# Three expert levels of a perceiver on one code: tokens gathered by expert, four pairs per level, TensorE branching by counts

## The chip, the cores and the metric

The kernel runs on one core of one Trainium2 chip. The metric is the device time of one execution in microseconds. Shown are three runs of the kernel before (672.74, 673.07 and 673.65, median 673.07) and one execution taken by the profiler.

Engines are named by their work: TensorE (PE: matmuls; PEld is its weight loading), VectorE (DVE), ScalarE (ACT), GpSimd (POOL), and SyncE (SP), which issues the transfers.

## The reference, cut to what matters

128 tokens (two batches of 64) of 256 values pass four levels. Each level is cross-attention to a context, then a mixer, then a feed-forward layer of eight experts of which every token uses two, and every part adds its output to x:

```python
x = x + _L1_ffn_ref(_layernorm(x), ...)
x = x + _L2_ffn_ref(_layernorm(x), ...)
x = x + _L3_ffn_ref(_layernorm(x), ...)
```

The feed-forward layer of level 2, for example:

```python
logits = xf @ router_w.T
top_w, top_i = lax.top_k(softmax(logits), 2)
top_w = top_w / sum(top_w)                 # combine[token, expert]
g = einsum('nd,ehd->neh', xf, w_gate)
u = einsum('nd,ehd->neh', xf, w_up)
y = einsum('neh,edh->ned', silu(g) * u, w_down)
out = einsum('ned,ne->nd', y, combine)
```

Level 1 has hidden width 1024, one product with a bias and Gelu (no gate), and an output bias. Level 2 has width 512, gate and up, Silu, no biases. Level 3 has width 1024, gate and up with biases, Silu, an output bias, and a router bias. All is float32. Level 0 (Gelu, dense in both kernels) is not touched.

## The kernel before, in words

All of x lies on 128 partitions, one token each. The stages follow one another: l0x, l0a, l0f, l1x, l1a, l1f, l2x, l2t, l2f, l3x, l3a, l3f (x: cross-attention, a or t: mixer, f: experts). A stage starts with the row normalisation of x and its transposition by TensorE, since TensorE contracts over partitions. `in_written_order` (L283) keeps each engine's instructions in the order of the text; elsewhere a scheduler orders them. Every engine works its own queue in order; SyncE does too, so a transfer whose buffer is not free holds all transfers behind it.

Weights come through a pool of buffers by size (L123): six of 1 MB ("w8"), four of 0.5 MB ("w4"), six small. `weight` (L125) takes the next free buffer and issues the load. `bank` (L88) gives one PSUM bank (512 float32 columns), `two_banks` (L91) a tile of two.

**Dense levels.** l1f (from L1773) and l2f (from L2366) compute all eight experts for all 128 tokens. `gate` (L331) makes the router's logits, the best two and their weights `comb`. For each expert `features` (L383) computes the hidden values turned (features on partitions), weights as the stationary operand; in l1f ScalarE applies Gelu with a bias column (L1784), in l2f ScalarE applies Silu to the gate and VectorE multiplies. `Mix.add` (L374) computes the output product and VectorE adds it, scaled by the token's weight (L378). `later` lets the output product of one expert stand behind the hidden product of the next.

**Gathered level.** l3f uses `experts` (L620). Tokens are sorted by expert into 128 slots per pair (r, r+4): a one-hot matrix `pick` made from the tokens' positions gathers x by a matmul (`gather`, L672), weights are now the moving operand and the gathered tokens the stationary one, so that the hidden values stand with slots on partitions, and `from_slot` (the transposed picks with the tokens' weights) scatters the outputs into one sum `acc` (L712). A pair has 64 slots for each of its experts, as two column tiles of TensorE; if the first expert of the pair has no token, all 128 slots go to the second. TensorE loads that decision from memory (`read_split`, L720) and branches (`by_tiles`, L725) for every hidden product (L643) and output product (L702). The hidden product is done in two halves of 512 columns, each with a gate and a product bank. Both halves lie in the same two tiles of two banks (`room_for_sums`, L631): the low banks of the two tiles are one half, the high banks the other. ScalarE applies Silu (L664), VectorE multiplies, TensorE turns the result (L688). `add_biases` (L653) opens the sums of the next pair with the biases by a small matmul.

Tokens beyond an expert's room go to four overflow blocks of 32 slots. `plan_blocks` (L836) is computed always, and 14 indirect loads on GpSimd always fetch those blocks' weights. Whether they are used is a branch at the end (L955) of TensorE, ScalarE and VectorE on `any_over`, read at L946.

**Constants and fillers.** `Counting` (L525) makes counting matrices with GpSimd and VectorE; it is set up before l3a, as is the negated sum of the router's columns (`less_sums`, TensorE and VectorE), with which the logits can be computed from x before it is normalised. `keep_busy` (L314) issues matmuls without use. Work for later stages is used as a filler too: in l1a and l1f TensorE computes values of level 3's cross-attention from `l3x_wv` (`context_values`, L403/L405), in l2t and l2f keys from `l3x_wk` (L429/L434). l3x_wk holds a "w4" buffer until level 3.

**l1a.** Its chain from the router-like logits to the new x is VectorE's: an addition (L1732), a maximum, ScalarE's exponential (L1735), six products and sums (L1745, L1749), then TensorE's turning of rows (L1756) and the product with x (L1764). TensorE runs fillers beside it.

Of the kernel before, what the change touches and what calls it, by code (L numbers as in the profile page):

```python
# [18 lines left out]
P = 128  # L19
# [18 lines left out]
    ("l1x_bq", 4), ("l1x_bk", 4), ("l1x_bv", 2), ("l1f_b1", 64),  # L38
# [20 lines left out]
def tile_perceiver(ctx: ExitStack, tc: tile.TileContext, i: dict, out: bass.AP):  # L59
# [465 lines left out]
    class Counting:  # L525
# [3 lines left out]
        def __init__(self, pool, biases):  # L529
# [30 lines left out]
            )  # L560

            self.p, self.p32 = p, p32
            self.biases = made(512, "bs")
            nc.sync.dma_start(self.biases, i[biases])

    class Shelf:
# [13 lines left out]
        def whole(self, t, wide):  # L580
            return lambda c, f: t[:, c * wide + f.start : c * wide + f.stop]

        def load(self, r):
            for n in self.order:
                src = i[f"{self.name}_w{n}"]
                _, _, chunks, wide = src.shape
                for j in range(2):
                    t = self.room(self.place(r, j, n), chunks * wide)
                    nc.sync.dma_start(t, src[r + PAIRS * j].rearrange("p c f -> p (c f)"))
                    self.at[r, j, n] = self.whole(t, wide)  # L590

        def fetch(self, blocks, index, index2):

            for j, n in blocks:
                src = i[f"{self.name}_w{n}"]
                _, _, chunks, wide = src.shape
                tag = self.place(OVER, j, n)
                parts = 2 if tag == "halves" else 1
                ts = []
                for k in range(parts):  # L600
                    t = self.room("w4" if parts == 2 else tag, chunks * wide // parts)
                    at = index[:, j : j + 1] if parts == 1 else index2[:, j, k : k + 1]
                    nc.gpsimd.indirect_dma_start(
                        t, None, src.rearrange("e p (k c) f -> (e p k) (c f)", k=parts),
                        bass.IndirectOffsetOnAxis(ap=at, axis=0),
                        bounds_check=8 * P * parts - 1, oob_is_err=False,
                    )
                    ts.append(self.whole(t, wide))
                each = chunks // parts
                self.at[OVER, j, n] = lambda c, f, ts=ts, each=each: ts[c // each](c % each, f)  # L610

    def tiles_of(k):

        if k == OVER:
            return [(slice(j * 32, j * 32 + 32), j) for j in range(4)]
        if k == 0:
            return [(slice(0, P), 1)]
        return [(slice(j * 64, j * 64 + 64), j) for j in range(2)]

    def experts(name, x, consts, shelf, blocks, pool, acc, less_sums, bias, b2):  # L620
        count, width = consts.count, 1024
        from_slot = pool.tile([P, OVER + 1, P], F32, name="from_slot")
        over, over_w = (pool.tile([P, P], F32, name=n) for n in ("over", "over_w"))
        own_over = pool.tile([P, P], F32, name="own_over")
# [3 lines left out]
        xg, hT, y, own, prods = {}, {}, {}, {}, {}  # L628
        low, high = slice(0, 512), slice(512, 1024)

        def room_for_sums():  # L631
            ps, other = two_banks(), two_banks()
            return [
                (ps[:, low], 1, low, 0), (other[:, low], 0, low, 2),
                (ps[:, high], 1, high, 1), (other[:, high], 0, high, 3),
            ]

        def hidden(r, parts, tiles):

            for part, n, f, k in parts:  # L640
                for c in range(2):
                    for s, j in tiles:
                        nc.tensor.matmul(  # L643
                            part[s], xg[r][:, c, s], shelf.at[r, j, n](c, f),
                            start=(r == 0 and c == 0), stop=False,
                            skip_group_check=True,
                        )

        def add_biases(r, parts):
            mine = own_over if r == OVER else own[r]  # L650
            for part, _, _, k in parts:
                e = slice(32 * k, 32 * k + 8)
                nc.tensor.matmul(  # L653
                    part, mine[e], consts.biases[e], start=(r > 0), stop=(r == 0),
                    skip_group_check=True,
                )

        def gates(r, parts):
            if r not in prods:
                prods[r] = pool.tile([P, width], F32, name="m_prod", bufs=2)  # L660
            g = pool.tile([P, width], F32, name="m_g")
            for k, (part, n, f, _) in enumerate(parts):
                if k % 2 == 0:
                    nc.scalar.activation(g[:, f], part, AF.Silu)  # L664
                else:
                    nc.vector.tensor_tensor(prods[r][:, f], part, g[:, f], ALU.mult)

        def gather(r):
            ps = bank()
            mine = over if r == OVER else pick[:, r]  # L670
            for c in range(2):
                nc.tensor.matmul(  # L672
                    ps[:, c * P : (c + 1) * P], xl[:, c * P : (c + 1) * P], mine,
                    start=True, stop=True,
                )
            if r == OVER:
                nc.tensor.transpose(ps[:, 2 * P : 3 * P], over_w, ident)
            xg[r] = pool.tile([P, 2, P], F32, name="m_xg", bufs=2)
            nc.scalar.copy(xg[r].rearrange("p c s -> p (c s)"), ps[:, : 2 * P])
            if r == OVER:  # L680
                nc.scalar.copy(from_slot[:, OVER], ps[:, 2 * P : 3 * P])

        def turn(r, k):
# [9 lines left out]
            if k:  # L693
# [16 lines left out]

        def scatter(r):
            nc.tensor.matmul(  # L712
                acc, from_slot[:, r], y[r], start=False, stop=(r >= PAIRS - 1),
                skip_group_check=True,
            )

        split = {}
# [7 lines left out]
        def by_tiles(r, behind, work):  # L725

            with tc.If(split[r] == 1) as shared:
                with in_written_order(behind):
                    work(tiles_of(1))
            with shared.Else():  # L730
                with in_written_order(behind):
                    work(tiles_of(0))

        with in_written_order() as done:
            ps = bank()
            for c in range(2):
                nc.tensor.transpose(ps[:, c * P : (c + 1) * P], x[:, c * P : (c + 1) * P], ident)
            keep_busy(1)
# [5 lines left out]
            r_ = rstd_of(mv[:, 1:2], 1, AF.Silu)  # L744
# [6 lines left out]
                lg, less_sums, mv[:, 0:1], ps[:, :8], ALU.mult, ALU.add  # L751
            )
            nc.vector.scalar_tensor_tensor(lg, lg, r_, bias, ALU.mult, ALU.add)
# [9 lines left out]
            )  # L763
            diff, th, w = stat(name="g_d"), stat(name="g_t"), stat(2, "top_w")
            nc.vector.tensor_tensor(diff, best[:, 0:1], best[:, 1:2], ALU.subtract)
            nc.scalar.activation(th, diff, AF.Tanh, scale=0.5)
            keep_busy(4)
# [3 lines left out]
            nc.tensor.matmul(ps[:, :8], consts.upto, mask, start=True, stop=True)  # L771
            keep_busy(2)
            one, two = slice(0, PAIRS), slice(PAIRS, 8)
            at_slot = pool.tile([P, 8], F32, name="m_at_slot")
            any_first = pool.tile([P, PAIRS], F32, name="m_any")
            split_at = small.tile([P, PAIRS], U32, tag="split", bufs=1, name="split")
            limit = pool.tile([P, 8], F32, name="m_limit")
            pos, number = (pool.tile([P, 8], F32, name=n) for n in ("m_pos", "m_number"))
            nc.vector.tensor_scalar(split_at, ps[:, 8 : 8 + PAIRS], 0.0, None, ALU.is_gt)
            nc.vector.tensor_scalar(any_first, ps[:, 8 : 8 + PAIRS], 0.0, None, ALU.is_gt)  # L780
            nc.vector.tensor_tensor(pos, ps[:, :8], mask, ALU.mult)
            nc.vector.scalar_tensor_tensor(
                at_slot[:, two], any_first, 64.0, pos[:, two], ALU.mult, ALU.add
            )
            nc.vector.tensor_tensor(at_slot[:, two], at_slot[:, two], mask[:, two], ALU.mult)
            nc.vector.scalar_tensor_tensor(
                at_slot[:, one], pos[:, one], 64.0, pos[:, one], ALU.is_le, ALU.mult
            )

            def picked(r):  # L790
                nc.vector.tensor_scalar(
                    pick[:, r], count, at_slot[:, r : r + 1], None, ALU.is_equal
                )
                nc.vector.scalar_tensor_tensor(
                    pick[:, r], count, at_slot[:, PAIRS + r : PAIRS + r + 1], pick[:, r],
# [3 lines left out]
            picked(0)  # L799
            read_split(0)  # L800
            nc.scalar.copy(number, ps[:, 8:16])
            gather(0)
            nc.vector.tensor_scalar(limit[:, one], any_first, 64.0, None, ALU.mult)
            nc.vector.tensor_scalar(limit[:, two], any_first, -64.0, float(P), ALU.mult, ALU.add)

            def owned(r):
                own[r] = pool.tile([P, P], F32, name=f"own{r}")
# [9 lines left out]
            for r in range(1, PAIRS):  # L817
                picked(r)
                owned(r)
# [6 lines left out]
            wide = pool.tile([P, PAIRS, P], F32, name="m_wide")  # L826
            for t, k in ((slot_w, 0), (wide, PAIRS)):
                for r in range(PAIRS):
                    e = slice(k + r, k + r + 1)
                    nc.vector.tensor_scalar(  # L830
                        t[:, r], count, at_slot[:, e], comb[:, e], ALU.is_equal, ALU.mult
                    )
            nc.gpsimd.tensor_tensor(slot_w, slot_w, wide, ALU.add)
# [1830 lines left out]
```

## Time and profile before

| | us |
|---|---|
| median of three runs | 673.07 |
| profiled execution | 673.79 |
| its span (first to last instruction) | 671.9 |
| l1f: x's transposes to those of l2x | 187.16 to 249.53 |
| l2f: first expert's product to l3x's transposes | 499.14 to 544.50 |
| l3f: first hidden product to the last scatter | 605.98 to 667.16 |

The mean granted clock of TensorE is 0.998. In the profile's lines an operation is told by its line in the kernel, its engine, its tiles (output <- input) and shape, and, in brackets, the idle time of its engine before it and what ended that. TensorE's records overlap each other by their pipelining, so distances are taken between starts. A float32 matmul leaves two matmul records and two weight-load records; TensorE has 4812 of each.

### The profile page before, as it was taken

How to read it: one execution, taken by the hardware profiler on the slowest of the kernel's cores; microseconds unless marked ns; L12 is line 12 of the kernel's file. 1: busy time of each engine (PE TensorE's matmuls, PEld its weight loads, DVE VectorE, ACT ScalarE, POOL GpSimd, SP SyncE). 2: the span in 40 equal slices, each digit the busy share in tenths (PEclk: the TensorE clock that was granted, in tenths of full speed). 3: DMA queues.
4: the chain of work that ended last, by engine and by line, in shares of the span. 5: the costliest groups of instructions: out<-in, count | busy, mean ns of one | idle time of the engine just before them, and what ended most of it. 6: DMA issues, size and time to landing. Idle time of an engine off the chain costs nothing. (4 is left out here: it accounts for less than half of the span.)

```text
span 671.9 us, 11767 instructions
## 1 busy us (share of the span) xinstructions
PE 638.5 (95%) x4812; PEld 506.3 (75%) x4812; DVE 297.8 (44%) x814; ACT 261.1 (39%) x531; POOL 62.6 (9%) x88
## 2 busy tenths in 40 slices
PE   7989999999899999999999989999999999989996
PEld 3547659766589988999997778999979966774443
DVE  5875451278420014554554435634422257755211
ACT  1464461488543332332323515305331159641111
POOL 3450000000000000000000040030000000100043
PEclk9999999999999999999999999999999999999999
DMA  8960025810038885000001300011118840274760
GB/s 285 401 270 1 17 72 199 322 44 1 3 125 299 289 267 210 2 1 1 1 1 58 131 1 1 2 63 63 63 63 301 299 151 2 90 303 186 318 250 10
DMA packets 21367, 86.81 MB, mean 129 GB/s; under 512 B 4080, under 2 KB 8704, under 8 KB 13024
## 3 DMA queue, kind: packets, MB, share of 16 engines
q1 hardware_dynamic: 19040, 85.96, 35.2%
q8 instruction: 41, 0.67, 0.4%
q0 software_dynamic: 2016, 0.01, 0.1%
q14 instruction: 14, 0.11, 0.0%
q10 hardware_dynamic: 256, 0.06, 0.0%
HBM read 98.46 MB, written 0.13 MB: 147 GB/s over the span
## 5 line engine op out<-in xcount | busy, mean ns | idle before, releaser
L1894 PE MATMUL bank<-l2x_ctx,p 128*128 128x193 f32 x256 | 48.1, 327 | 0.0
L378 DVE SCALAR_TENSOR_TENSOR x_new<-bank,comb,x_new 128x256 f32<-128x256 f32 x24 | 11.6, 484 | 80.0 <-PE bank L270 80.0
L1894 PEld LDWEIGHTS bank<-l2x_ctx,p 128*128 128x128 f32 x256 | 40.8, 190 | 0.4
L1547 DVE CUSTOM_DVE_ANT_0 p<-two_banks,zero 128x1024 f32<-128x1024 f32 x32 | 38.6, 1217 | 5.2 <-PE two_banks L1537 5.0
L1555 ACT ACTIVATE p<-p,negmax 128x1024 f32<-128x1024 f32 x32 | 36.9, 1153 | 4.7 <-DVE negmax L1547 4.7
L1843 PE MATMUL two_banks<-l2x_qA,ctxA 128*128 128x128 f32 x256 | 31.9, 278 | 0.0
L1858 DVE TENSOR_REDUCE l2x_mx<-two_banks 128x128 f32<-128x1024 f32 x16 | 19.6, 1224 | 26.6 <-PE two_banks L1850 26.6
L1843 PEld LDWEIGHTS two_banks<-l2x_qA,ctxA 128*128 128x128 f32 x256 | 30.3, 192 | 1.2 <-issue 1.0
L1784 ACT ACTIVATE l1f_hT<-bank,cols 128x128 f32<-128x128 f32 x64 | 18.2, 367 | 32.9 <-PE bank L270 32.9
L270 PEld LDWEIGHTS bank<-xT,l1f_w_sb 128*128 128x128 f32 x256 | 29.7, 192 | 0.6 <-issue 0.3
L270 PE MATMUL bank<-xT,l1f_w_sb 128*128 128x128 f32 x256 | 30.1, 276 | 0.0
L270 PEld LDWEIGHTS bank<-xT,l2f_w_sb 128*128 128x128 f32 x256 | 29.6, 192 | 0.3
L270 PE MATMUL bank<-xT,l2f_w_sb 128*128 128x128 f32 x256 | 29.8, 275 | 0.0
L270 PE MATMUL bank<-l1f_w_sb,l1f_hT 128*128 128x256 f32 x128 | 28.8, 379 | 0.0
L1880 DVE TENSOR_TENSOR p<-two_banks,l2x_shift 128x512 f32<-128x512 f32 x32 | 20.6, 686 | 13.1 <-ACT l2x_shift L1875 13.1
L270 PEld LDWEIGHTS bank<-l1f_w_sb,l1f_hT 128*128 128x128 f32 x128 | 23.8, 190 | 2.9
L1887 ACT ACTIVATE p<-p 128x512 f32<-128x512 f32 x32 | 19.6, 630 | 12.1 <-DVE p L1880 12.1
L1562 PEld LDWEIGHTS two_banks<-ident,p 128*128 128x128 f32 x128 | 13.7, 140 | 11.0 <-ACT pT L1591 9.1
L223 ACT ACT_TABLE_LOAD x16 | 20.5, 1283 | 0.3
L1537 PE MATMUL two_banks<-n_kT,n_qx 32*128 32x512 f32 x128 | 19.2, 640 | 0.0
L1562 PE MATMUL bank<-ident,p 128*128 128x128 f32 x128 | 18.6, 280 | 0.5
L1850 PE MATMUL two_banks<-l2x_qB,ctxB 64*128 64x128 f32 x256 | 18.6, 285 | 0.0
(598 smaller groups left out, 1313.0 us busy)
## 6 DMA issues: line engine op xcount, KB each, us to landing
l1f_w_sb<-in_l1f_w_dram SPq DMA_DIRECT2D x16, 1024.0 KB, 4.8
l3f_w_sb<-in_l3f_w_dram SPq DMA_DIRECT2D x12, 1024.0 KB, 5.3
more_w<-in_l3f_w_dram SPq DMA_DIRECT2D x12, 1024.0 KB, 8.2
l0f_w_sb<-in_l0f_w_dram SPq DMA_DIRECT2D x8, 1024.0 KB, 8.9
l2f_w_sb<-in_l2f_w_dram SPq DMA_DIRECT2D x8, 1024.0 KB, 4.8
l2f_w_sb<-in_l2f_w_dram SPq DMA_DIRECT2D x8, 512.0 KB, 4.5
xh<-in_ctx_dram SPq DMA_DIRECT2D x8, 192.0 KB, 6.0
l2x_ctx<-in_ctx_dram SPq DMA_DIRECT2D x1, 1536.0 KB, 8.0
```

The lines of the kernel that those rows point to most:

```text
L223: nc.scalar.activation(junk, behind, func, scale=0.0)
L270: nc.tensor.matmul(dst, lhsT, rhs, start=(k == 0), stop=(k == len(pairs) - 1))
L1537: nc.tensor.matmul(sc[u][:, n * 512 : (n + 1) * 512], qx[c, n][rows_, b].rearrange("p h q -> p (h q)"), kT[c, b][rows_, n, :], start=True, ...
L1547: nc.vector.tensor_tensor_reduce(p[u], sc[u], zero.to_broadcast([P, NK]), -1.0, 3.0e38, ALU.add, ALU.min, least)
L1555: nc.scalar.activation(p[u], p[u], AF.Exp, bias=sc[u], scale=-1.0, accum_out=total[u // 4][:, u % 4 : u % 4 + 1],)
L1562: nc.tensor.transpose(ps[:, kc * P : (kc + 1) * P], p[u][:, (4 * k + kc) * P : (4 * k + kc + 1) * P], ident,)
L1843: nc.tensor.matmul(sc[k][:, n, t, :], ctxA[:, b, n, t * P : (t + 1) * P], qA[:, j, b].rearrange("p h q -> p (h q)"), start=(t == 0), stop= ...
L1850: nc.tensor.matmul(sc[k][:, n, t, :], ctxB[half[n], b, t * P : (t + 1) * P], qB[half[n], j, b].rearrange("p h q -> p (h q)"), start=False, ...
L1858: nc.vector.tensor_reduce(mx[k], sc[k].rearrange("p n t q -> p q (n t)"), AX.X, ALU.max)
L1880: nc.vector.tensor_tensor(p[k][:, n], sc[k][:, n], shifts[k].unsqueeze(1).to_broadcast([P, 4, P]), ALU.add,)
L1887: nc.scalar.activation(p[k][:, n], p[k][:, n], AF.Exp)
L1894: nc.tensor.matmul(po[k][:, : CD + 1], p[k][:, kc // 4, kc % 4, :], crows[:, b * 8 + kc, :], start=(kc == 0), stop=(kc == 7),)
```

## The change

- l1f and l2f use `experts` as l3f does. A `Level` tells the activation, the width, whether there is a gate, and the biases. In l1f and l2f a pair is shared 64/64 when its first expert has more than 32 tokens, else 32/96, the latter in four 32-column tiles (three of them for the second expert). l3f keeps 64/64 or whole.
- The sums of a half lie in the two banks of one tile, the second half's in another tile. `acc` is an ordinary bank.
- `Counting` and the router sums of levels 1 to 3 are made before and in l1a instead of l3a; the sums' matmul and negation are written behind two fillers and ahead of the addition that starts l1a's chain.
- The overflow plan, its loads and its products are all inside two branches at the end of each level.
- Weights of l2x, l3x and l3f's first pair are asked for earlier in the text, behind the shelf of l1f or l2f. l1f has four 1 MB buffers more ("more").

```diff
-    def tiles_of(k):
-        if k == OVER:
-            return [(slice(j * 32, j * 32 + 32), j) for j in range(4)]
-        if k == 0:
-            return [(slice(0, P), 1)]
-        return [(slice(j * 64, j * 64 + 64), j) for j in range(2)]
+    class Level:
+        def room_for_sums(self):
+            low, high = slice(0, 512), slice(512, 1024)
+            ps = two_banks()
+            if self.width == 512:
+                return [[(ps[:, low], 1, low, 0), (ps[:, high], 1, high, 1)]]
+            if not self.gated:
+                return [[(ps[:, low], 1, low, 0), (ps[:, high], 1, high, 1)]]
+            other = two_banks()
+            return [
+                [(ps[:, low], 1, low, 0), (ps[:, high], 0, low, 2)],
+                [(other[:, low], 1, high, 1), (other[:, high], 0, high, 3)],
+            ]
+        def tiles_of(self, equal):
+            if equal:
+                return [(slice(j * 64, j * 64 + 64), j) for j in range(2)]
+            if self.least == 0:
+                return [(slice(0, P), 1)]
+            return [(quarter_tile(j)[0], min(j, 1)) for j in range(4)]
...
-            ps, other = two_banks(), two_banks()
-            return [
-                (ps[:, low], 1, low, 0), (other[:, low], 0, low, 2),
-                (ps[:, high], 1, high, 1), (other[:, high], 0, high, 3),
-            ]
...
-        with tc.If(more == 0) as none:
-            pass
-        with none.Else():
-            with in_written_order():
-                gather(OVER)
...
+        given = None
+        for part in (lambda _: over_features(), over_outputs):
+            with tc.If(some == 0) as none:
+                pass
+            with none.Else():
+                with in_written_order():
+                    given = part(given)
...
+        def router_sums(self):
+            ps = bank()
+            at = SMALL["l1f"][0]
+            accumulate(ps[:, :24], [(ones, routers[:, c, at : at + 24]) for c in range(2)])
+            nc.vector.tensor_scalar(self.less_sums, ps[:, :24], -1.0, None, ALU.mult)
...
         steps(fill[1])
         steps(fill[2], 2)
+        consts.router_sums()
...
-        mix = Mix(x, gate(xlT, "l1f"))
-        for e in range(8):
-            w1 = weight("l1f_w1", e)
-            w2 = weight("l1f_w2", e)
...
+    shelf.load(0)
+    nc.sync.dma_start(l1f_bs, i["l1f_bs"])
+    for r in range(1, PAIRS):
+        shelf.load(r)
+    l2x_w = [weight(f"l2x_w{n}") for n in "qkvo"]
+        def fill_l1f(k):
+            if k == 0:
+                steps(fill[3])
+            keep_busy((1, 4, 2, 1)[k])
+        x = experts(
+            Level("l1f", AF.Gelu, 1024, False, 32, biases=l1f_bs, b2=l1f_b2),
+            x, shelf, pool, None, fill_l1f,
+        )
...
+    shelf = Shelf("l2f", (1, 2), lambda r, n: "w8" if n == 1 else "w4")
+    for r in range(PAIRS):
+        shelf.load(r)
+    l3x_w = [weight(n) for n in ("l3x_wq", "l3x_w1", "l3x_w2", "l3a_wz", "l3a_wh")]
+    last_shelf = Shelf("l3f", (1, 0, 2), lambda r, n: "more" if r % 2 else "w8")
+    last_shelf.load(0)
+        last = kv3.keys(1, 0)
+        def fill_l2f(k):
+            if k < 3:
+                steps(last, (3, 1, 0)[k])
+            keep_busy((0, 4, 2, 1)[k])
+        x = experts(Level("l2f", AF.Silu, 512, True, 32), x, shelf, pool, pool, fill_l2f)
```

In one round of `experts` TensorE's order is, after the change as before: hidden product of pair r, gathering of pair r+1, output product of pair r-1 (called out_of(r-1) below), turning of pair r, biases of pair r+1, scatter of pair r-1.

## The prediction

> **What bounds the kernel now.** I read the page first (busy shares, costliest groups), then TensorE's timeline in the stages that the diff touches, then SyncE's issues and the branch instructions.
>
> ```profile
> PE 638.5 (95%) x4812; PEld 506.3 (75%) x4812; DVE 297.8 (44%) x814; ACT 261.1 (39%) x531; POOL 62.6 (9%) x88
> ...
> L378 DVE SCALAR_TENSOR_TENSOR x_new<-bank,comb,x_new 128x256 f32<-128x256 f32 x24 | 11.6, 484 | 80.0 <-PE bank L270 80.0
> ...
> L1784 ACT ACTIVATE l1f_hT<-bank,cols 128x128 f32<-128x128 f32 x64 | 18.2, 367 | 32.9 <-PE bank L270 32.9
> ```
>
> TensorE is busy 95% of the span, and in the dense expert stages VectorE (80.0 us idle) and ScalarE (32.9) wait for it. So a microsecond of matmuls saved there is a microsecond of time, as long as nothing else becomes late.
>
> TensorE's timeline in l1f, l2f and l3f (start, duration, line; overlapping groups, so I subtract starts; one fp32 matmul leaves two records and two weight loads):
>
> ```profile
> 188.58 3.82 PE L270 MATMUL bank<-xT,l1f_w_sb 128*128 128x128 f32 x32
> ...
> 246.25 1.03 PE L403 MATMUL two_banks<-l3x_wv_sb,ctxA 128*128 128x256 f32 x4
> ...
> 249.53 0.44 PE L260 MATMUL bank<-ident,xl 128*128 128x128 f32 x2
> ```
>
> ```profile
> 605.98 3.70 PE L643 MATMUL two_banks<-l3f_w_sb,m_xg 128*128 128x512 f32 x8 [0.46 <-ACT m_xg L679]
> ...
> 611.50 3.67 PE L643 MATMUL two_banks<-l3f_w_sb,m_xg 128*128 128x512 f32 x8 [0.77 <-ACT m_g L664]
> ...
> 620.46 3.65 PE L643 MATMUL two_banks<-more_w,m_xg 128*64 128x512 f32 x16
> ...
> 653.15 3.65 PE L643 MATMUL two_banks<-more_w,m_xg 128*64 128x512 f32 x16 [0.50 <-ACT m_g L664]
> ```
>
> The second answer holds the argument for the change: 16 records of 64 columns take 3.65 us where 8 of 128 columns take 3.67. Two experts side by side, 64 tokens each, cost what one expert with 128 tokens costs. It also shows two waits (0.77, 0.50) of one half's sums for the evacuation of the other half in the same banks.
>
> **Routing.** With the reference's inputs the experts get l1f 57 0 41 9 | 7 19 51 72, l2f 34 5 16 41 | 1 75 42 42, l3f 0 3 26 58 | 109 0 54 6 tokens. So l1f's pairs 0 and 2 and l2f's 0 and 3 go 64/64, the others 32/96 in four 32-column tiles; none overflows, and every overflow block is jumped over.
>
> **l1f: -8.2.** Today: x's transposes at 187.16, next stage's transposes at 249.53. After: the logits end about 188.8 (router row 188.11 + 0.65), and from there routing is exposed; in l3f the logits end at 600.21 + 0.65 = 600.86 and the first hidden product starts at 605.98, 5.11 later, so here the first hidden product starts at 193.9 (today 188.58). A round costs l3f's round with half its hidden product: hidden 3.55, gather 0.6, outputs 3.6, turning 1.0, biases 1.06, scatter 0.65, together 10.5; round 0 is 3.6 + 4.8 (biases, ways back, gather, turning; 615.11 to 620.46 in l3f less one filler), round 1 has 0.35 more (start of the sum), the last 3.55 + 11.1 (l3f from 656.63 to x_new's end 667.71). That gives 202.3, 213.2, 223.7 and x_new at 238.3 (today 246.9). The 3.3 us of key filler now stand behind a second jump, 0.2 later: 241.3. I take the four-tile groups at the price of two; the attention shows 32-column tiles side by side:
>
> ```profile
> 170.02 2.07 PE L1607 MATMUL two_banks<-pT,n_v 128*32 128x128 f32 x64
> ```
>
> 64 records in 2.07 less a 0.27 tail is 0.11 for four, the interval of one 128x128 record. [...]
>
> **l2f: -6.9 by TensorE alone, -1.0 with its weights.** x is transposed at 495.6 and the key filler (2.87) now runs before the router, so the logits come at about 499.5, the first hidden product at 504.6 (today 499.14). Rounds: 5.8 (hidden 3.58; activation, product and turning 2.2), 7.15, 7.15 (3.58 + 0.6 + 1.8 + 0.5 + 0.65) and 10.2 to x_new: 534.9 against 542.3, less 0.5 because the filler after the stage stands behind the second jump. But SyncE issues in order, and w2 of this stage has three free buffers of four (l3x_wk holds one; today's fourth load is issued at 508.29, after expert 0's output):
>
> ```profile
> 93.82 0.33 SPq L132 DMA_DIRECT2D l2f_w_sb<-in_l2f_w_dram  x1
> ...
> 130.76 3.25 SPq L132 DMA_DIRECT2D l2f_w_sb<-in_l2f_w_dram  x2
> ```
>
> The eighth w2 tile can be issued only when out_of(2) has ended. By TensorE alone hidden(3) ends at 528.2, out_of(2) at 530.0, and out_of(3) starts at 531.4; the tiles that wait for out_of(0) and out_of(1) already make these about 1 later. SyncE has put two 1 MB tiles of l3f ahead of the eighth (issued at hidden(3)'s end, 529.2). Rows: 1 MB lands 4.75 after its issue, one queued behind it 2.4 later, 0.5 MB 1.33. So those land at 533.9 and 536.1 and the eighth at about 537.3; unqueued, 0.5 MB took 3.45 (from 93.82), which bounds it below at 531 + 3.45 = 534.5. I take 537.3; outputs, copy, scatter and x_new are 3.6 more (as in l3f from 662.32, less 1.8): 540.9, 5.9 above TensorE's own 534.9, and the next stage 1.0 earlier than today. If queues share the engines, the delay is nothing to 3.
>
> **l3f: -1.4.** Gone: 0.77 and 0.50 (separate banks; next late is then the matmul itself), and about 0.2 of small vector operations before the first gather. The 14 indirect loads (0.99 each on GpSimd) and 25 plan operations on VectorE lie beside TensorE today: nothing. Second jump -0.1.
>
> **l1a: +4.05.** The router sums move from l3a here, written behind two fillers of l3x_wv. Their VectorE negation stands ahead of the addition L1732 that starts l1a's chain, and VectorE is in order:
>
> ```profile
> 178.71 0.19 DVE L1732 TENSOR_TENSOR l1a_moved<-bank,rows 128x32 f32<-128x32 f32 x1 [0.79 <-PE bank L270]
> 178.94 0.19 DVE L1734 TENSOR_REDUCE l1a_nm<-l1a_moved 128x1 f32<-128x32 f32 x1
> ```
>
> The filler ends at 181.8, the four sum records last 0.63 (router row 177.98 to 178.61), wait 0.1, negation 0.17: the addition starts at 182.75 instead of 178.71. Behind it wait eight vector operations, ScalarE's exponential, L1756 and L1764. Today the chain is already late for TensorE (idle 0.64 before L1756, 0.52 before L1764), so all 4.05 reach the end. Bounds: 0 (if it were ordered after the addition) to 4.05. The constants' three GpSimd and four VectorE operations (0.24 + 0.29 + 0.14, 4 x 0.2) end before L270's wait at 173.72.
>
> **Jumps.** TensorE jumps over each overflow block only after its own last matmul has ended. Rows of branch instructions in l3f:
>
> ```profile
> L955 PEldq COMPARE_BRANCH  x2: 63/1808/3552, 666.5 to 667.3; - x2
> ...
> L727 PEldq COMPARE_BRANCH  x21: 63/174/380, 604.8 to 663.7; - x21
> ```
>
> L727's 21 branches pass at most 64 records and take 0.06 to 0.38. The jump over L955's block (80 matmuls, 4 records each, 320) took 3.55, today behind the output's transfer. After, there are six jumps, over 84 and 164 records in l1f, 76 and 84 in l2f, 156 and 164 in l3f. Bounds 0.06 to 3.55 each; I take 0.2, counted above, since these are nearer to 64 than to 320. [...]
>
> **Sum.** -8.2 - 1.0 - 1.4 + 4.05 = -6.55. The profiled execution took 673.79 (span 671.9), 0.7 above the median 673.07: 667.2 there, **666.5** against the median.
>
> **Rivals.**
> 1. *l2f's w2 is not late* (queues share, or the buffer is free earlier): 5.9 more, 660.6. Against: l3f_w of 511.86 lands at 516.62 and the 0.5 MB of 513.59 1.33 behind it, one after the other. Chance 0.17.
> 2. *The jumps fetch*: five exposed jumps (two in l1f, two in l2f, l3f's first; the last is behind the output) at 3.55 instead of 0.2 are +16.8, 683.3, **slower** than before. It decides from 1.8 us a jump (666.5 + 5 x 1.6 = 674.4). For it: L955's row, and TensorE's queue is empty at each. Against: the blocks are half as long. Chance 0.2 (0.16 of it slower).
> 3. *Four 32-column tiles with 512 columns run two at a time*: l1f's two pairs +14.3, l2f's +10.7 less the stall, about 687. Against: L1607. 0.05.
> 4. *l1a does not wait* (the negation is hidden): 662.5. 0.06.
>
> **How the numbers follow.** Forecast as summed, 664 to 671: 0.52. Range 8 in 10: 660 takes in rival 1 and 4; up to 678 takes in jumps of about 2.5. A change under 0.2% (1.35 us) can't be told from none here. Faster: 0.52 + 0.17 + 0.06 and a little of rival 2: 0.77. Same 0.02. Slower 0.16 + 0.05: 0.21.
>
> **What would show it.** l1f's hidden products at about 198 (with l1a's 4), 10.5 apart, and four-tile groups of 3.6 us; TensorE idle about 4 before the l1a row turning, released by VectorE; a wait of TensorE for a DMA of l2f's last w2 tile, 4 us; no waits on m_g in l3f; overflow jumps under 0.5. Wrong if a jump shows microseconds, if 32-column groups take 7 us, or if weights of l1f come late.

## The result

The changed kernel takes **680.6 us** (median of four executions, 677.9 to 683.3) against 673.4 beside it: a ratio of **1.0107 [1.0065, 1.015]**, so it is slower by some 1%. Forecast were 666.5 us, 660 to 678. The profiled execution took 681.47 (span 679.8), where the working gave 667.2: the miss is 14.3 (14.4 by the spans).

The profile page of the changed kernel, the rows of the same kind as before (busy time, clock in 40 slices, code fetched) and one group:

```profile
PE 628.8 (93%) x4752; PEld 457.3 (67%) x4752; DVE 303.9 (45%) x844; ACT 254.6 (37%) x499; POOL 49.9 (7%) x76
...
PEclk9999999999889989999999999999999979999999
...
q8 instruction: 46, 0.75, 0.4%
...
L725 PE MATMUL bank<-l2f_w_sb,m_hT 128*32 128x256 f32 (+1 forms) x96 | 11.4, 421 | 7.4 <-DMA l2f_w_sb<-in_l2f_w_dram 7.3
```

TensorE's work shrank as meant: 9.7 us less busy, 7.9 us more span. The second line is new: the granted clock falls in four slices (before it fell only behind the last matmul). The last group waits 7.3 us for weights.

TensorE's waits, longest first (line, releaser: us in all, times, longest), name the places:

```profile
PE bank L725 <- DMA l2f_w_sb<-in_l2f_w_dram: 7.3, 3, 5.7
...
PE bank L1819 <- DVE l1a_rows L1812: 3.9, 1, 3.9
PE bank L739 <- issue: 3.6, 1, 3.6
...
PE bank L800 <- DVE m_m L789: 1.7, 1, 1.7
```

"Issue" in the third means that nothing in the profile released it. The busy time and mean clock by stage, for the changed kernel's l1a, l1f's routing, its rounds, its end, and l2f's end:

```profile
176.04:193.81 17.77, 12.88 (x48) 7.68 (x49) 4.70 (x15) 2.80 (x7) 0.00 (x0) 0.71 0.43 180
193.81:202.36 8.55, 5.77 (x33) 4.23 (x31) 4.92 (x26) 4.89 (x9) 0.00 (x0) 1.00 0.00 0
202.36:243.00 40.64, 39.95 (x323) 19.42 (x327) 8.80 (x31) 9.20 (x20) 0.75 (x1) 1.00 0.55 209
243.00:255.30 12.30, 8.18 (x67) 4.57 (x59) 1.61 (x5) 3.44 (x5) 0.85 (x2) 0.86 0.95 303
...
527.00:555.50 28.50, 19.93 (x126) 8.31 (x122) 4.38 (x9) 5.75 (x10) 0.72 (x1) 0.88 0.75 292
```

After the stretch and its length come the busy times of TensorE, its weight loads, VectorE, ScalarE and GpSimd, then the clock: 0.71, 0.86 and 0.88 at three places, 1.00 in l1f's routing and rounds. The last two numbers are the share of the DMA engines that was busy and GB/s.

Stage by stage, from one stage's transposes of x to the next's (l2 is the stage l2t with l2f, because x of l2f is transposed behind other work before, and ahead of it now):

| stage | before | after | difference | forecast |
|---|---|---|---|---|
| l1a | 10.14 | 17.77 | +7.63 | +4.05 |
| l1f | 62.37 | 61.49 | -0.88 | -8.2 |
| l2 | 174.63 | 179.89 | +5.26 | -1.0 |
| l3f | 67.55 | 65.59 | -1.96 | -1.4 |
| behind l3f | 5.09 | 3.79 | -1.30 | 0 |
| all else | 352.1 | 351.2 | -0.9 | 0 |

So three stages carry the miss. (The 0.9 of the last row lies ahead of l1a.) In l1a, TensorE's timeline of the changed kernel (start, duration, line; in brackets the idle time before and what ended it):

```profile
177.47 1.11 PE L403 MATMUL two_banks<-l3x_wv_sb,ctxA 128*128 128x256 f32 x4
...
179.47 2.07 PE L403 MATMUL two_banks<-l3x_wv_sb,ctxA 128*128 128x256 f32 x4
181.48 1.01 PE L405 MATMUL two_banks<-l3x_wv_sb,ctxB 64*128 64x256 f32 x4
182.42 0.62 PE L270 MATMUL bank<-routers,ones 128*128 128x24 f32 x4
186.91 0.48 PE L1819 MATMUL bank<-ident,l1a_rows 64*64 64x64 f32 x4 [3.86 <-DVE l1a_rows L1812]
...
188.89 1.91 PE L403 MATMUL two_banks<-l3x_wv_sb,ctxA 128*128 128x256 f32 x4
```

The wait of 3.86 is the one that was forecast. Beside it the same filler L403 takes 1.11, then 2.07, then 1.91: half clock, which is what a granted clock of 0.50 is called from here on.

At the end of l1f, and at l2f's last output product:

```profile
242.70 2.80 PE L725 MATMUL bank<-l1f_w_sb,m_hT 128*32 128x256 f32 x48
249.14 0.70 PE L739 MATMUL bank<-m_y,from_slot 128*128 128x256 f32 x2 [3.64 <-issue]
250.32 2.02 PE L403 MATMUL two_banks<-l3x_wv_sb,ctxA 128*128 128x256 f32 x4 [0.49 <-PEq L1019]
...
255.30 0.44 PE L260 MATMUL bank<-ident,xl 128*128 128x128 f32 x2
```

```profile
537.37 1.93 PE L725 MATMUL bank<-l2f_w_sb,m_hT 128*32 128x256 f32 x30 [1.13 <-DMA l2f_w_sb<-in_l2f_w_dram]
...
540.66 0.65 PE L725 MATMUL bank<-l2f_w_sb,m_hT 128*64 128x256 f32 x2
547.04 3.67 PE L725 MATMUL bank<-l2f_w_sb,m_hT 128*64 128x256 f32 x14 [5.74 <-DMA l2f_w_sb<-in_l2f_w_dram]
```

The last 14 records take 3.67 where 30 (of 32 columns) took 1.93: half clock again, behind the wait. The jump over the first overflow block in l1f, a branch instruction of TensorE (min, median, max in ns; first and last start):

```profile
L1019 PEldq COMPARE_BRANCH  x1: 3342/3342/3342, 245.7 to 245.7; - x1
```

The record of a fetch of 16 KB of TensorE's code begins at 246.33, 0.59 into this jump, and TensorE resumes 2.8 later. The second jump of l1f took 0.184.

### The profile page after: what moved, and what is told of

Its sections match the earlier page's. It is cut to its first block, busy times and chain, and to the rows that moved or that the text cites. A ratio compares the mean times of both kernels' runs of the same rounds, so it can differ in the third digit from the quotient of the medians.

```text
span 679.8 us, 11726 instructions
## 1 busy us (share of the span) xinstructions
PE 628.8 (93%) x4752; PEld 457.3 (67%) x4752; DVE 303.9 (45%) x844; ACT 254.6 (37%) x499; POOL 49.9 (7%) x76
## 5 line engine op out<-in xcount | busy, mean ns | idle before, releaser
L717 DVE COPY m_hT<-bank 128x512 f32<-128x512 f32 x12 | 8.3, 692 | 50.4 <-PE bank L711 50.4
L691 ACT ACTIVATE m_g<-two_banks 128x512 f32<-128x512 f32 x12 | 7.2, 598 | 51.0 <-PE two_banks L668 42.1
L692 DVE TENSOR_TENSOR m_prod<-two_banks,m_g 128x512 f32<-128x512 f32 x12 | 8.3, 691 | 39.6 <-ACT m_g L691 39.6
L319 PE MATMUL bank<-ctxA,ones 128*128 128x256 f32 x88 | 22.7, 386 | 0.1
L732 ACT COPY m_y<-bank 128x256 f32<-128x256 f32 x12 | 4.5, 372 | 45.0 <-PE bank L725 24.8
L1204 POOL TENSOR_SCALAR xh<-xh,cx_mv,rstd 128x192 f32<-128x192 f32 x16 | 17.2, 1090 | 14.9 <-DVE rstd L231 14.9
L725 PE MATMUL bank<-l2f_w_sb,m_hT 128*32 128x256 f32 (+1 forms) x96 | 11.4, 421 | 7.4 <-DMA l2f_w_sb<-in_l2f_w_dram 7.3
L668 PE MATMUL two_banks<-more_w,m_xg 128*64 128x512 f32 x80 | 18.0, 597 | 0.0
```

The costliest lines, as they stand in the source:

```text
L319: nc.tensor.matmul(ps[:, :D], ones, ctxA[:, 0, 0, :D], start=True, stop=True)
```

## The theory after the result, and its rivals

Four losses, taken as separate: VectorE's negation in l1a (forecast), ScalarE's eviction in l1f's routing (its copy of a filler's sums out of PSUM, L510), code that comes late at one jump, and l2f's weights; and behind each wait a stretch of half clock, which no term of the sum had. The rivals: the half clock is caused by something else (the DMA traffic) and the waits cost only their own time; the "issue" wait is not code; the gain of l1f isn't there at all, because 32-column tiles or the branches eat it. Each experiment changes one thing in the changed kernel, later ones in the best version.

## Experiments

**1. Router sums behind l1a's last reduction.**

```diff
-        consts.router_sums()
         steps_of = [1, 4, 16]
...
             nc.vector.tensor_reduce(dst, terms, AX.X, ALU.add)
+        consts.router_sums()
```

> The router sums' matmul and negation are moved behind the last reduction of l1a's chain; nothing else. Theory (the negation holds VectorE behind the filler): the addition that starts the chain goes back to about 1.6 us after the router row, TensorE's idle time before the turning of rows falls from 3.86 to at most 1 us, and from xl's transposes to those of l1f it takes 10.2 to 12 us (17.77 after the change, 10.14 before it); a half-clock stretch of 3.4 us that came ahead of the wait may remain. Whole kernel 5.5 to 7.5 us less, about 674. Rival (the stage is slow because of the half clock or of the weight transfers that now run beside it, not because of the wait): the wait goes but the fillers stay slow, 3 us less at most. The position of the overflow jumps in the code is unchanged, so l1f's jump stays at about 3.3 us.

678.5 us, ratio 1.007 [1.0038, 1.0102]. TensorE's l1a in this kernel:

```profile
181.92 0.62 PE L270 MATMUL bank<-routers,ones 128*128 128x24 f32 x4
182.48 0.33 PE L1819 MATMUL bank<-ident,l1a_rows 64*64 64x64 f32 x4
183.32 0.67 PE L1827 MATMUL bank<-xl,bandT 128*128 128x256 f32 x2 [0.52 <-DVE bandT L1825]
183.83 1.03 PE L403 MATMUL two_banks<-l3x_wv_sb,ctxA 128*128 128x256 f32 x4
```

The wait is gone, and so is the half clock behind it (L403 1.03); l1a takes 11.57. But the kernel gained 2.1, not 6.2: l1f took 63.5 (3.41 of half clock in its routing, where the changed kernel had none, a jump of 3.30 and 6.83 of half clock behind it) and l2 181.7, where the last output product had 13.65 of half clock around it instead of 6.83. What is saved ahead is partly lost in the later waits, which stay.

**2. l2f's output weights of pairs 1 and 2 in four buffers of their own.**

```diff
-    shelf = Shelf("l2f", (1, 2), lambda r, n: "w8" if n == 1 else "w4")
+    w2_scope = ExitStack()
+    shelf = Shelf(
+        "l2f", (1, 2), lambda r, n: "w8" if n == 1 else "more" if r in (1, 2) else "w4",
+        w2_scope.enter_context(stage_pool(name="l2f_more", bufs=4)),
+    )
...
+    w2_scope.close()
```

> l2f's output weights of pairs 1 and 2 get four buffers of their own, so that the tiles of pair 3 are issued early; nothing else. Theory (the eighth tile is late): TensorE waits for no l2f output tile (0.43, 1.13 and 5.74 us after the change), the half clock behind the long wait goes (14 output records in 3.67 us go to 1.9), and from the last projection of l2t to l3x's transposes it takes 46 to 48 us (55.56 after the change, 50.62 before it). Whole kernel 7.5 to 9.5 us less, about 672. Rival (all weights of this stage together are too much for the queue, so that the wait only moves to the hidden products' weights or to l3x's): half of that or less, with a new wait for a transfer in l2f or l3x.

668.67 us, ratio 0.9929 [0.9907, 0.9952]. No wait for l2f's weights is left, and no half clock in l2. SyncE's issues in the changed kernel, and in this one (the eighth w2 tile is the lone "x1" of l2f_w):

```profile
535.71 0.81 SPq L598 DMA_DIRECT2D l3f_w_sb<-in_l3f_w_dram  x2
539.33 0.33 SPq L598 DMA_DIRECT2D l2f_w_sb<-in_l2f_w_dram  x1
```

```profile
517.35 0.80 SPq L598 DMA_DIRECT2D l3f_w_sb<-in_l3f_w_dram  x2
519.86 0.33 SPq L598 DMA_DIRECT2D l2f_w_sb<-in_l2f_w_dram  x1
```

It is issued 15.3 ahead of its use (535.12) where the changed kernel was ready for it 1.3 after the issue (540.66). l2 takes 169.06, 10.8 less; from the start of each waiting output product to the next group it is 1.0, 1.7 and 8.1 shorter. This confirms the mechanism and gives its full price, clock included. The kernel gained 11.9, more than the 7.5 to 9.5 expected; in the profiled execution l1a (15.67) and l1f (60.00, its jump 1.89) were shorter too, though the edit doesn't touch them.

**3. A filler in l1a's wait**, to part the clock from the wait.

```diff
         consts.router_sums()
+        keep_busy(8)
```

> Eight matmuls without use (3.45 us at full clock) are put behind the router sums, into TensorE's wait of 3.86 us in l1a. Theory (the clock falls because TensorE was idle): the wait's end stays where it was, the clock is full from the turning of rows to l1f's transposes, and that stretch takes 4.7 us as before the change instead of 6.90; 2.2 us less in this stage. Rival (the half clock comes from something else, as the first half-clock stretch that stands ahead of the wait): no gain here. The 33 instructions more also move the overflow jumps: if the jump's cost is a matter of its place in the code, l1f's 3.34 us may fall below 0.5; if it is not, it stays.

680.97 us, ratio 1.0104 [1.0086, 1.0121]. l1a takes 15.57 instead of 17.77: with TensorE busy through the wait, the fillers behind it run at 1.03 and 0.70 again. TensorE's filled wait and the filler behind it:

```profile
182.40 3.70 PE L319 MATMUL bank<-ctxA,ones 128*128 128x256 f32 x16
...
187.84 1.03 PE L403 MATMUL two_banks<-l3x_wv_sb,ctxA 128*128 128x256 f32 x4
```

So the half clock behind the wait follows from the idle time. The stage's time alone would not show it: experiments 2, 4 and 5 leave l1a's code as it is, wait included, and took 15.66 to 15.73. But in each of them a stretch of 6.83 begins in the wait (at 183.39 to 183.92), and here none does. One stretch of 3.4, ahead of the wait, stayed. Unplanned: the 33 instructions more moved TensorE's code, and the slow jump was gone.

```profile
L1019 PEldq COMPARE_BRANCH  x4: 68/126/305, 244.0 to 247.0; - x4
```

l2 was worse (182.7; 13.65 of half clock), and a new stretch of 6.83 began at 197.78 in l1f's routing, behind an idle time of 1.74, so that l1f still took 59.50 with the jump gone. The kernel gained nothing.

**4. Code moved, nothing executed more.**

```diff
+                    if name == "l1f" and r == 0 and not shelf.shifted:
+                        keep_busy(16)
+                        shelf.shifted = True
```

The added lines stand in the branch of l1f's first pair that this data doesn't take.

> Sixteen matmuls without use are added to a branch that these inputs do not take (l1f, pair 0, shared 32/96), so nothing more is executed but 65 instructions stand ahead of the later jumps. Theory (the 3.34 us of l1f's first overflow jump are the fetching of a code block that had not been asked for, because the earlier jump went over the block's beginning): the jump takes less than 0.5 us, the half clock behind it goes, l1f is 3 to 5 us shorter; another jump may become slow in its place. Rival 1 (the jump is slow because weights of l2x fill the transfer queues at that moment): still about 3.3 us. Rival 2 (it waits for the length of the jump, 84 records): still about 3.3 us.

684.13 us, ratio 1.0149 [1.0117, 1.0181]. No jump over 0.4 is left, but TensorE stops in the middle of a filler, with its operands long there:

```profile
247.19 0.48 PE L405 MATMUL two_banks<-l3x_wv_sb,ctxB 64*128 64x256 f32 x1
251.01 1.22 PE L405 MATMUL two_banks<-l3x_wv_sb,ctxB 64*128 64x256 f32 x3 [3.34 <-issue]
```

A fetch of code begins at 248.47, 2.5 ahead of the resume. So the wait is one for code, not for the branch's condition or for data; moving the code moved it. The other half of the theory failed: l1f took 62.60, not 3 to 5 us less. Transfers of weights beside it are not needed for such a wait: the last jump of l3f in the changed kernel took 2.2 with the DMA engines 17% busy, and ended 2.4 after the start of its fetch record; in l1f, with 98%, it was 2.8.

**5. ScalarE's eviction behind the softmax.**

```diff
-            if k == 0:
+            if k == 1:
                 steps(fill[3])
```

> One edit in the changed kernel: the filler in l1f's routing, with the eviction of its sums by ScalarE, stands behind the router's softmax instead of ahead of the features' root. Theory (ScalarE's eviction of 1.0 us and the table load 1.3 us in order ahead of the root make the logits late): the 1.74 us idle time of TensorE before the means' product in l1f goes, first hidden product 1.0 to 1.85 us earlier after x's transposes (8.55 to 6.7 to 7.5), kernel 678.5 to 680. Rival (TensorE's filler itself is what routing waits for, or the table load alone): 8.55 stays within 0.3, kernel 680.6 within its spread. Waits for l2f's output weights and the long jump of 3.3 us in l1f are untouched by both.

681.24 us, ratio 1.0116 [1.0101, 1.0132]. x's transposes are at 192.26 and the first hidden product at 199.05: 6.79 instead of 8.55, and the row "L800 <- DVE m_m" of the waits is gone. The theory holds for the stage (1.76). The total doesn't show it (678.5 to 680 were expected): it lies within the spread of the changed kernel, and l2 grew by 0.7.

**6. The three mends together** (1, 2 and 5).

> The changed kernel with three edits together: router sums behind l1a's last reduction, l2f's output weights of pairs 1 and 2 in buffers of their own, ScalarE's eviction in l1f's routing later. If the losses are separate and add up: 668.7 (own buffers) less 6.2 (l1a 17.8 to 11.6) less 1 to 1.85 is 660.6 to 661.5. Rival (what is gained in l1a is given back in l1f by half-clock stretches and by the wait for code at the first overflow jump, as when the sums alone were moved): 664 to 667. The jump over the first overflow block in l1f still takes 1.9 to 3.4 us by both.

**661.8 us, ratio 0.9812 [0.9795, 0.983]**: faster than both kernels. l1a 10.25, l2 169.0; the losses do add up: 660.6 to 661.5 were expected of that, and the executions run from 659.3 to 662.4. The half clock is down to one stretch of 3.41, at l1f's end, where the jump still takes 3.13 and TensorE idles 3.42.

**7 and 8. Without branches, and without the overflow blocks only.** From 6; the first writes out the arrangement that this data needs.

```diff
-            with tc.If(split[r] == 1) as shared:
-                work(level.tiles_of(True))
-            with shared.Else():
-                work(level.tiles_of(False))
+            work(level.tiles_of(equal_here == 1))
...
-        for part in (lambda _: over_features(), over_outputs):
-            with tc.If(some == 0) as none: ...
```

> The kernel with the three edits, and without any branch: each level's pairs are written out in the one arrangement that this data needs, and the overflow blocks and the reading of counts are left out, so it computes rightly for this data alone. Theory (TensorE pays for the branches mostly by late code, 3.3 us at one jump in l1f, about 2.4 at the last jump and 1.7 by half clock behind the first, and little by the others): 5 to 8 us less than the kernel with three edits, 653 to 657, no idle of TensorE over 1 us behind l1f's last scatter. Rival (the long jump is only where TensorE waits for something else, such as the filler's weights or the gather): less than 2.5 us less, and an idle time of 2 to 3 us stays at l1f's end. Second rival (each of some 40 jumps and 12 register reads costs 0.2 or more on the path): 10 us or more less.

> The kernel with the three edits, without the overflow blocks (they are jumped over for this data, so it computes rightly only where no expert overflows), the choice between 64/64 and 32/96 or whole still by branches. Theory (late code comes where a jump goes over a code block's beginning and a second one follows before it is caught up): the 3.3 us go or shrink with the two overflow jumps in l1f, 2 to 6 us less than the kernel with three edits. Rival (the choices' branches alone bring the late code): less than 1.5 us less, and a wait of TensorE of 2 to 3.4 us for its code stands elsewhere within l1f or behind it.

653.2 us, ratio 0.9699 [0.9684, 0.9714], without any branch; 655.94, ratio 0.9742 [0.9727, 0.9757], without overflow. l1f's end in 6 and in 8:

```profile
233.71 3.45 PE L725 MATMUL bank<-l1f_w_sb,m_hT 128*32 128x256 f32 x60
240.58 0.70 PE L739 MATMUL bank<-m_y,from_slot 128*128 128x256 f32 x2 [3.42 <-issue]
241.71 2.03 PE L403 MATMUL two_banks<-l3x_wv_sb,ctxA 128*128 128x256 f32 x4 [0.44 <-PEq L1019]
...
246.69 0.44 PE L260 MATMUL bank<-ident,xl 128*128 128x128 f32 x2
```

```profile
232.68 3.23 PE L725 MATMUL bank<-l1f_w_sb,m_hT 128*32 128x256 f32 x56
236.47 0.70 PE L739 MATMUL bank<-m_y,from_slot 128*128 128x256 f32 x2 [0.56 <-ACT m_y L732]
237.01 1.03 PE L403 MATMUL two_banks<-l3x_wv_sb,ctxA 128*128 128x256 f32 x4
...
240.29 0.44 PE L260 MATMUL bank<-ident,xl 128*128 128x128 f32 x2
```

From the scatter L739 on, the same work is 6.1 in one and 3.8 in the other, and the scatter itself comes 2.9 sooner after the last product: l1f is 59.48 against 54.32. So the two overflow jumps cost 5.2 there, the half clock behind them included, and 0.9 in l2f. The 5.9 by which 8 beats 6 are what its theory expected (2 to 6). The remaining branches and register reads together: l1f 54.32 to 53.66, l2f 42.15 to 41.96, l3f 65.52 to 64.91, 1.6 of span (2.7 by the medians). The second rival (0.2 or more each, 10 in all) falls. 8.6 for all branches is a little over the 5 to 8 of the theory; in the profiled executions 1.4 of the difference stands ahead of l1a, where the two kernels are alike. No execution of 7 shows half clock (mean granted clock 1.00 in all four), with the weights' transfers still in place, so the rival that blames these transfers for the clock falls too. The executions of 7 spread over 0.5 us, where those of the changed kernel spread over 5.3.

**9 to 12. What makes the code late?** All from 6; 9 joins both overflow parts in one block, 10 and 11 move the code by 16 and 48 instructions as in 4, 12 by 36 and then 52. Where a block of code begins no run shows: what theory 1 below makes of each position is the author's estimate.

```diff
-        for part in (lambda _: over_features(), over_outputs): ...
+        with tc.If(some == 0) as none: pass
+        with none.Else():
+            over_outputs(over_features())
```

> The kernel with the three edits, and in each level both parts of the overflow in one block, so that TensorE has one jump over some 235 of its instructions instead of two over 85 and 151. [...] Theory 1 (code comes late where one jump has gone over a beginning and the next does not): no jump over 0.6 us in l1f and no idle over 1 us behind its last scatter, 655.5 to 658. Theory 2 (the longer the jump, the likelier it waits for code): the one jump takes 3 us or more, 661 to 663. Of the two jumps in each level one goes: 0.1 to 0.3 us a level by both.

660.76 us, ratio 0.9803 [0.9789, 0.9817]. The one jump took 1.86, TensorE idled 2.11 over it, and a stretch of half clock followed:

```profile
239.76 1.93 PE L403 MATMUL two_banks<-l3x_wv_sb,ctxA 128*128 128x256 f32 x4 [2.11 <-issue]
```

Theory 1 falls (1.86 is over its 0.6), and so does theory 2 (3 or more): the jump over 235 instructions took less than that over 85 (3.13 in experiment 6). The sum stays.

> The kernel with the three edits, and 16 TensorE instructions in a branch of l1f that is not taken for this data, so that nothing is executed more and all code behind stands 16 further. [...] Theory 1 (late code where one jump has gone over a beginning and the next does not): the jump of 3.1 us becomes less than 0.6, no half-clock stretch behind it, 655.5 to 658. Theory 2 (the wait belongs to the jump as such, to its length or to an empty queue): it stays at 2 to 3.4 us, 660 to 663.

661.35 us, ratio 0.9816 [0.9792, 0.984]: against theory 1 again.

```profile
L1023 PEldq COMPARE_BRANCH  x1: 3252/3252/3252, 236.4 to 236.4; - x1
```

> As the run with 16 instructions in a branch that is not taken, but 48. [...] Theory 1: a wait of TensorE of 2 to 3.5 us for its code stands in l1f's end again, at a jump or in straight code behind it, as where the code stood 65 further; 659 to 663. Theory 2 (only the first alignment was unlucky, any shift heals it): no such wait, 655.5 to 658.

662.95 us (one execution). No jump over 0.76, a wait of 1.47 in the filler's straight code, which is less than theory 1 asked for and more than theory 2; a stretch of half clock in l1a and another at l1f's end.

> The kernel with the three edits, and 36 TensorE instructions in the branch of l1f's first pair and 52 in the branch of its last product, neither taken for this data, so that nothing more is executed. [...] Theory 1 of the earlier runs (one jump of two goes over a beginning) fell: 16 instructions more left the jump at 3.25 us, 33, 48 and 65 more did not. [...] Rival (the overflow jumps wait as such, because TensorE's queue is empty there, or code is late wherever it is): 2 to 3.5 us of jump or idle time at l1f's end, l1f 57 to 61, kernel 659.5 to 663.

666.11 us, ratio 0.9902 [0.9883, 0.9921], slower than 6. The position was chosen for jumps under 0.6 us and 656 to 658.5 in all, by the author's estimate of when the next code is asked for, which no run shows. It failed: the first overflow jump is quick (0.30 at most), the second is the worst of all, beyond the rival's 2 to 3.5 too.

```profile
L1025 PEldq COMPARE_BRANCH  x1: 5223/5223/5223, 238.6 to 238.6; - x1
```

Its fetch record begins only 2.7 into the jump, and l1f took 62.22. **Open**: which instruction or event asks for the next 16 KB. What seven arrangements of the same code show is that one of l1f's last jumps, or the straight code behind them, waits 1.5 to 5.5 us in six of them; only 33 more (experiment 3) had no such wait. TensorE resumes 2.4 to 2.9 us after the fetch record begins in all of these. Moving the filler ahead of the jumps wasn't tried.

## Why the prediction was wrong, step by step

The mechanisms named were nearly all there; four steps failed: the price of the jumps ("I take 0.2", and one took 3.34), the routing time carried over from l3f (1.8 short), the size of l2f's wait (5.9 for 10.8), and a term left at nothing without a reason, the granted clock, which is 7.3 of the 14.4 and lies in part inside the others.

- **l1a, "+4.05"**: the wait came as worked out (3.86, released by the last reduction). It measured +7.63 because of the term that wasn't there: half clock on the fillers around it (2.07 and 1.91 for 1.03 to 1.13), 3.6 us: 2.2 of them, behind the wait, go in experiment 3, and 1.3, ahead of it, are what l1a takes longer in experiment 1 than in 6. The stretch ahead is chance: with the same code in l1a, experiments 2, 4 and 5 have none there and take 15.66 to 15.73, so some 2 of the +7.63 belong to this one execution.
- **Jumps, "I take 0.2"** between 0.06 and 3.55: this step failed at one jump. Four of the six took 0.17 to 0.29, the last (2.2) lay behind the output. The first in l1f took 3.34, and with the half clock behind it 5.2 (experiment 6 against 8). The choice by length was wrong: this jump skips 85 instructions (the prediction had 84), and the one right behind it, over 151 (the prediction had 164), took 0.18. Rival 2 had the mechanism, at five jumps; it was one.
- **"The first hidden product starts" 5.1 after the logits, as in l3f**: off by 1.8. In l3f ScalarE had loaded its table 2.8 ahead of the root (L228) and idled; in l1f the filler's eviction (1.01) and then the table load (1.28) are ahead of the root:

```profile
193.93 1.01 ACT L510 COPY n_v<-two_banks 128x1024 f32<-128x1024 f32 x1 [6.25 <-PE two_banks L405]
...
194.96 1.28 ACT L228 ACT_TABLE_LOAD   x1
...
196.25 0.30 ACT L228 ACTIVATE root<-bn_mv,eps 128x1 f32<-128x1 f32 x1
```

The step carried over a row from a stage with another queue in front of it. Experiment 5 gives the 1.76 back.
- **l1f, "-8.2"** was right but for these: without jumps and with the eviction moved, l1f is 54.32, 8.05 below before. Rounds of 11.15 and 10.53 against 10.9 and 10.5.
- **Four 32-column tiles at the price of two**: right. In experiment 2, one hidden product of each kind:

```profile
507.75 3.65 PE L668 MATMUL two_banks<-l2f_w_sb,m_xg 128*64 128x512 f32 x16 [0.46 <-ACT m_xg L704]
...
513.67 3.64 PE L668 MATMUL two_banks<-l2f_w_sb,m_xg 128*32 128x512 f32 x32 [0.16 <-issue]
```

Twice the records in the same time (3.64 against 3.65), so rival 3 (7 us a group) falls.
- **l2f, "-6.9 by TensorE alone"**: -5.6 (experiment 2). Of the 1.3 that are missing, 0.8 lie between the first hidden product and x_new (steps of 5.92, 7.29, 7.27 and 10.64 against 5.8, 7.15, 7.15 and 10.2); the key filler, which now runs behind x_new instead of beside it, costs 0.8 where 0.5 had been taken. **"5.9 above TensorE's own"**: the right wait, 10.8 in size. The output products of pairs 1 and 2 lost 2.7 instead of 1, so the eighth tile was issued 3.7 after hidden(3)'s end instead of 1.8; it landed 7.7 after its issue instead of 6.3 (by the prediction's own rows 537.7, not 537.3), behind l3f's two tiles (issued at 535.71, landed at 543.3 and 545.8); and half clock added 2.0 on the last product (3.67 for 14 records, where 16 took 1.95 in experiment 2).
- **l3f, "-1.4"**: -1.96; the waits on m_g are gone, as said.
- **The missing term**, the granted clock: about 3.6 in l1a, 1.7 in l1f and 2.0 in l2f, 7.3 of the 14.4. The profile of before could not show it, since TensorE's longest idle time between two matmuls there is 0.82; but the two waits that the forecast added, in l1a and l2f, were of microseconds. Half clock set in within the waits of 3.86 and 5.74 and 1.27 behind that of 3.64; shorter ones did it too (last section). A price for half clock at the two forecast waits would have been 2.2 and 2.0 of this term, but only the runs gave it; the long jump and the stretch ahead of l1a's wait were not foreseen.

By stages: 3.6 (l1a), 7.3 (l1f: 5.2 + 1.8 + 0.3), 6.3 (l2: 4.9 + 1.3), less 0.6 (l3f) and about 2.2 outside. Proven by taking away are the weights (2), the negation's wait (1), the eviction (5) and the overflow jumps (8). That half clock follows idle time is shown by 3; why it began at 178.73, behind two short waits of 1.19 together, is open.

## What to carry to other kernels

The waits of 3.64, 3.86 and 5.74 us that the change put into stages bound by TensorE cost their length and then more by half clock, 1.7 to 2.2 us each: price both, count shorter waits that stand close together as one (0.67 and 0.52, 1.19 in all, were enough once), and fill the wait or take it away before counting gains elsewhere. Before carrying a duration from one stage to another, list what stands ahead of it on each in-order queue there, ScalarE's evictions and table loads too (1.01 and 1.28 here). A jump's price isn't read from its length (3.34 over 85 instructions, 0.18 over 151); blocks that are never executed cost 5.2 us in l1f and 0.9 in l2f here, so measure the kernel without them once.

## What the runs showed of the hardware

- In the changed kernel half clock begins at 178.73, 185.56, 250.41 and 543.96: all apart by whole multiples of 3.413 us (2, 19 and 86), and its stretches last 3.41 or 6.83 (up to 13.65 in experiment 1). In every profiled execution with several stretches the starts lie on one such grid, at a different phase in each. The phase is a likely reason for the changed kernel's spread of 5.3 us beside 0.5 without waits (experiment 7); that link is argued, not shown.
- Half clock follows TensorE's idle time summed over one window of that grid (3.413 us), not the length of one wait. The stretch at 178.73 had no idle time above 0.67 ahead of it, but 1.19 in all in the window before it; the other three had 2.51, 2.62 and 2.76. Laid on their grids, the eleven executions with several stretches have 15 windows at full clock with 1.77 us or more of idle time, and half clock followed all 15; of 22 with 1.18 to 1.74 it followed 11; of 2011 with less it followed none. Half clock then stayed for another window in all 20 cases where 0.50 us or more of its window were idle, and ended in all 26 with 0.49 or less. Why one window between 1.18 and 1.74 tips and another doesn't is open.
- Code can be late without a jump: 3.34 in experiment 4, in a filler. The wait at a jump doesn't follow its length: the jump of 85 instructions took 3.34 in the changed kernel and 3.13 in experiment 6, the one of 151 behind it in the changed kernel 0.18, and the one of 235 in experiment 9 took 1.86. Neither theory 1 or 2 of experiments 9 to 11 nor the position chosen in 12 foretold the next wait.
